# An order of 4345 steps, its first 1753 arranged anew

## The chip, the cores and the metric

The kernel runs on one core of a Trainium2 chip. The metric is the device time of one execution in microseconds: the median of three runs of the kernel before is 1051.68 us (1048.98 to 1051.96). A profiled execution gives the start and end of every instruction on the five engines: TensorE (PE, with its weight loads as PEld), VectorE (DVE), ScalarE (ACT), GpSimd (POOL) and SyncE (SP), which issues every transfer of this kernel.

## What is computed

A transformer block on x of shape (8, 512, 512): attention with 16 heads of width 32 and a causal mask, then a feed-forward layer with quantised activations and ternary weights.

```python
x = x + layernorm(attention(layernorm(x)))      # eps 1e-5
x = x + layernorm(ffn(x))

# attention: q, k, v = split(x @ w_attn + b_attn), rotary turn of q and k that depends on the head
p = softmax(where(causal, q @ k.T, -inf)) * 512**-0.5
out = (p @ v) @ w_proj + b_proj

# ffn: two "bitlinear" layers with a gelu between (512 -> 2048 -> 512)
xn = layernorm(x)                                # eps 1e-6
x_hat = clip(xn * 128 / absmax(xn), -128 + 1e-6, 128 - 1e-6) * absmax(xn) / 128
w_hat = sign(round(w / (mean(abs(w)) + 1e-6))) * mean(abs(w))
y = x_hat @ w_hat.T
```

## The kernel before

The batch has eight images of 512 rows; rows are worked in tiles of 128, so there are 32 row tiles (b, c). Products that need more than half precision are formed from a high and a low f16 part, in three passes or with both parts as operands. The work is written as Python generators, one for each piece of work, and a letter names the stream that a generator belongs to. Each `yield` ends a *step*: a few instructions, mostly of one engine.

- `n`, `N`: load a row tile (`load_x`, L491), normalise it, split it in halves and transpose it (`prepare_x`, L496). In the first image PE transposes; later a transfer does, into xT.
- `w`, `H`, `J`, `B`, `R`, `I`: load and prepare the weights of attention. `t`, `T`, `Y`: load the sixteen pieces of the two feed-forward weights (`load_piece`, L406), sum their magnitudes (`magnitude`, L426) and make them ternary (`ternarize`, L461), half of it on DVE.
- `Q`: queries and keys of four heads (`queries_keys`, L565), twelve steps for one group, six of them for each of two PSUM tiles: matmuls (L575), eviction on ACT (L587) and DVE (L589). `V`: values of half the heads for a row tile (`values`, L538), four steps: two of matmuls (L545), ACT (L558), DVE (L560).
- `S`: scores of four heads (`maxima`, L596), nine steps for one block: three matmul steps (L610), each followed by two DVE steps (L624) that add the mask, take the extremum and empty PSUM into the tile p.
- `A`: probabilities (`probabilities`, L646): exponentials on ACT (L661), a cast to f16 on ACT (L667), the difference on POOL (L669), and then a transposing transfer of ph into pT. Each block has four such transfers, two of 128x24x128 and then two of 128x16x128 elements.
- `W`: the weighted sum of values (`weighted`, L682), seven steps for a pair of heads; the third and sixth read the smaller pT (L696). `G`: gather four heads, split and transpose them into oT. `r`, `P`: load the residual rows and project (`project`, L736; eight steps for a row tile, matmuls L741).
- `F`: the first quantisation (`ff_front`, L792), whose transfer makes qT of 128x8x128. `X`: the expansion (`ff_expand`, L817): matmuls L827, gelu on ACT L836. `Z`: the second quantisation (`ff_quantise`, L845), with two transfers of 128x16x128 into qT. `C`: the contraction (`ff_contract`, L876), fourteen steps for a row tile: eight of matmuls (L883), then statistics, output row and its store.

A letter and a number mean a step of a stream, counted from 0: A331 is the 332nd step of stream A.

What sets the order is the string `ORDER` (L36), 4345 letters. The kernel goes through it and lets the named stream take its next step; `pin` (L952) then ties every instruction to the one before it on the same engine, so that each engine executes in exactly this order:

```python
for k in "".join(ORDER.split()):
    step(k)
```

So an engine that waits holds up all that stands behind it in its own queue, and nothing else. SP's queue has loads, stores and transposing transfers in one line. Buffers are few: two PSUM tiles for the products of Q, V, P and C (`mm`), three larger ones for scores and the expansion (`sc`), three score tiles p, two each of ph and pT in either size.

All transposing transfers are issued here (L521):

```python
def transpose(dst, q):
    nc.sync.dma_start_transpose(
        out=dst.rearrange("p h k q -> p (h k) q"), in_=q.rearrange("p h f -> p (h f)")
    )
```

Of the kernel before, what the change touches and what calls it, by code (L numbers as in the profile page):

```python
# [33 lines left out]


ORDER = """  # L36
nNNNwHIwHHHNwJJNJNNnNHJBBBBBBBBBNNNNRHJJwRRRNNBNBnNHHHNNHHRwJJtHJNNJHRBtnNwwJNJtRHHBBRNNHRNNTJTH
JHJJNNTNRtNtTTtTtTHNNQHQQQQHJnJNtTJHNwYHQYYHYNYQYJQQQHwBYYHQtYYHQJJQHYYQQJSSBTQYYQSQQYYQQHQSSAAQ
AAQVYAAVtVJtYAAAttSSVAQYQAQtQSAAQQQAQJSAAQAABBQQAAAVJSVVAAAQJSAVSVVVVJRVVSAVVVVSAAAVAVnrSVTSQQVA
TVQVAAWNSnQVVQAQWrWWVnWWnQAAAVVTAVQTQQNNNNAWWWWWSWANAWVNNNAAAAAASNNNNNWSSRAATAQAAAASNAWWQNASAANA  # L40
VNVVWWWASGGAAASSWWSWWWWWWAAAAVVVGVAVSVSASNAVVVVAAANAANAWQAAQQQSQSAAAnQGQQGAAWQGSSSQWWWWAAVQAAQVS
WWWWWWWAAVAAAAAQWVAAQRRRRRRQSSAQSSAtWWWQAtASQSQQQAWAQWGGWWWGAVArAWQWQWWWWWASSASAQAVQTQVAATYVQYYY
GGGSSAAAAQQYYYYQQQSQAAAQYAAAPPPPPQPYWPWSSPVPAVPWVVFWWWWPPnAVPASFSFAAAASAAASPVVVAYPYAAAFFQQQQSSQW
WWFWWQWAAAASWAQQAAFAAYQQVSVNNYPSAAANVAVFSYQXAAANNNFAFAAXXXNXNXXAFFXQrnXXGPPFSSNNPPNWGWPVWNNWWAWA
WWVWWWWSPAAAAWVVAAAAVVVASZSYANNNAASFVYVVZArPYYPVAZXWZAAAVFnXXXXXFPXZAAXPXXSSAAAZZZQPGQPQSSWPSQQF
GWZWQQWSWQWAGWAZWWZQWQAWQWCGWZACAQAAQAWSSSAAZAAAQQQQQACAGAAAGASZZCWCWCSAAAVCVVGAAZCSSVQCSCWCWFWQ
WSWQWQAWWWWAAAAACVCWVQQFAAVQSVVZQWVAAASPVVPGQWSZAQQQQFGGNPQAZSSCQAAPQAAQQWWWWNWAAZZXZZVnXWAVANVV
AAAAPSAZXVFFPFZVVPSPNAZZnXASQSWQWWVQWQWAAPWPAZQAAWAQXQQQSQNNCQNSFNXCSAXQAXNnNANAASSFFXPZAXPZZWNr
NANSNNFCWWAWWWCPnGCZGWFPWCPPFWAANWWCZAAANWNWNSPSZZAAAVCVVVCWACAAZACXSCFXVXVXVVPQFSVQSAFFFZVAAAVQ
VZNSFZZXPXAAQQQQXFXQXFAXNQSZPQWPWSPXPWXCCZQWWZZAZZAPCAXFAACQWZPAAZCAPrXCAXZSFZFFZPPCFPSPSCPCXGGC  # L50
XXGWWWWWWGAAXASZZCCACPZWVZANCCCCZrVFCZXSFZVVZWCASQCZWAQAAAAACAQGAAFGSCQQCSCQQWNQWWWZWZZGSAAQCPXA
WQWWWWWWXAPCAAAAACCVSAAQWFZXVVGQVVFSXVSSXVVCrGVZFZXPGVPXSXPFZFFAZAVVQAPQASPAPQAAAAAAAAAWWSQQQQnZ
ZFXXCQCZQAZZCQQCSSCWFWFWWWCAAWWQWWWASCZVWPAVAACWZVSFVQCQnXPZAQFSAXXAZQAAZCZCACCSPASSAPAACASACAZA
XQAAQPXZXPXXPCXPQWWZZFGCZZWQWWQWGXZAZWQXCFAZAXWCWCAWWAWWCPrFNFNXNCQPQVCANAXFZnPFFNXVXNNWSNNAXZZX
ZCCZCSCPNVNCXCPVSSrNZCPnZZZZNCXAXAPZZAZZAFXACAPVNCNNAVSAPSZCXASZCVAVAAAVCZAAZSSAAVVCVSQZPCCASAAA
AXCQCWWSQVCPQVXXWQQWXQWVFVNWQCrPAZQPZZZQPGGGXAPGFZZAQWSQXAQPSCWWAWQWWWACQASNXFACFZZFQCAAASWFCZWW
CAAZAQFQQCGGSXCFQWPWZZZXWWPSAAAAAGAQNFACXACAQAZWSFFFXCSACVWWVnWWWZAAQSQPFXXZZWVXXWAAGVVNXFXSQZAG
FXAQVVSQAGSSZQXXZQCCZVVQZAAAAZQFVQAXSQVVAWFCFFQAZCWZACQAQPCPZXSCSCWPCWPCASXWrAZWZAZZPZZXXZAAAAFA
# [986 lines left out]
```

## Time and profile before

| what | value |
|---|---|
| median of three runs | 1051.68 us (1048.98 to 1051.96) |
| the profiled execution | 1051.51 us |
| its span, first to last instruction | 1049.7 us |
| mean granted PE clock | 0.978 |
| PE busy | 977.2 us, 93% |
| ACT busy | 904.8 us, 86% |
| DVE busy | 855.8 us, 82% |
| POOL busy | 759.7 us, 72% |
| transfers from SP's queue, share of 16 DMA engines | 90.2% |
| transposing transfers | 284: 128 into pT, 96 into qT, 32 into oT, 28 into xT |

The busy time of an engine is the time in which an instruction of it runs; waiting for a semaphore or issuing a transfer is not busy. For a transfer the profile gives two times: how long SP's queue was held by its issue, and when it landed. Step 1753 of the order, the first behind the rearranged part, starts on PE at 414 us of the span.

### The profile page before, as it was taken

To read this page: it belongs to the slowest core of one execution; us is meant where nothing else is said; L and a number is where in the kernel's file an instruction comes from. 1 tells how busy PE (TensorE), PEld (TensorE's weight loads), DVE (VectorE), ACT (ScalarE), POOL (GpSimd) and SP (SyncE) were. 2 spreads that over 40 slices of the span, in tenths; PEclk is the share of its full clock that TensorE was granted. 3 is DMA by queue.
4 is the path that set the end of the run, shared out by engine and by line. 5 is a ranking of instruction groups with operands and counts; after the bars stand their busy time and mean duration, and the time that the engine had idled before them with its cause. 6 is when DMAs were issued, how large, how long until landed. Compare 5 with 4: busy or idle time off the path is not lost.

```text
span 1049.7 us, 22994 instructions
## 1 busy us (share of the span) xinstructions
PE 977.2 (93%) x8258; PEld 511.0 (49%) x8258; DVE 855.8 (82%) x2674; ACT 904.8 (86%) x1502; POOL 759.7 (72%) x608
## 2 busy tenths in 40 slices
PE   5787888899999999999999999999999999999995
PEld 4544544445555555555545455454454454544442
DVE  7898789989998888887988897888778888866752
ACT  5789998999999998999899999889999889964552
POOL 5249875888877778877888688677967678865544
PEclk9898899999999999999999999999999999999998
DMA  9369998999999988999999999989999879995553
GB/s 308 111 143 205 185 222 128 183 185 194 192 188 181 163 177 163 201 176 183 178 196 177 170 192 178 167 160 192 185 169 175 171 142 170 198 193 110 110 101 80
DMA packets 585027, 181.10 MB, mean 173 GB/s; under 512 B 564304, under 2 KB 568400, under 8 KB 584912
## 3 DMA queue, kind: packets, MB, share of 16 engines
q1 hardware_dynamic: 584912, 179.63, 90.2%
q8 instruction: 64, 1.05, 0.4%
q14 instruction: 51, 0.42, 0.1%
HBM read 29.64 MB, written 8.39 MB: 36 GB/s over the span
## 4 chain that ended last, share of the span: by engine, by line
PE 26%; ACT 25%; DVE 18%; DMA 11%; POOL 10%; issue 9%; SPq 1%; POOLq 0%; ACTq 0%; DVEq 0%
PE sc L827 7%; ACT p L661 6%; PE mm L883 6%; DVE p L624 5%; POOL ph L669 4%; DMA pT<-ph 4%; DMA qT<-q 4%; PE mm L575 4%; ACT ph L667 3%; PE mm L545 2%; PE sc L696 2%; ACT junk L865 2%; ACT h L836 2%; PE mm L741 2%; ACT L836 2%
## 5 line engine op out<-in xcount | busy, mean ns | idle before, releaser
L669 POOL TENSOR_TENSOR ph<-p,ph 128x768 f16<-128x768 f32 (+1 forms) x192 | 355.7, 1856 | 112.8 <-ACT ph L667 92.6
L624 DVE CUSTOM_DVE_ANT_0 p<-sc,mask,e_scale 128x384 f32<-128x384 f32 (+3 forms) x512 | 255.4, 546 | 25.1 <-POOL ph L669 13.2
L883 PE MATMUL mm<-wout,qT 128*128 128x512 fp8e4 x1024 | 260.1, 383 | 6.6 <-ACT row L901 5.1
L827 PE MATMUL sc<-wfc,qT 128*128 128x512 fp8e4 x1024 | 254.6, 379 | 3.9 <-DVE low L624 1.9
L661 ACT ACTIVATE p<-p,nmax 128x384 f32<-128x384 f32 (+3 forms) x512 | 253.5, 552 | 3.0 <-DVE nmax L635 2.5
L575 PE MATMUL mm<-xT,wqk 128*128 128x512 f16 x768 | 203.6, 384 | 2.2 <-DVE vt L560 1.3
L667 ACT CAST ph<-p 128x768 f16<-128x768 f32 (+1 forms) x192 | 172.4, 898 | 5.0 <-DMA pT<-ph 2.0
L827 PEld LDWEIGHTS <-qT 128*128 128x128 f16 x1024 | 96.6, 98 | 117.6 <-issue 9.7
L883 PEld LDWEIGHTS <-qT 128*128 128x128 f16 x1024 | 95.1, 98 | 115.3 <-issue 15.3
L696 PEld LDWEIGHTS <-pT 128*128 128x128 f16 x2560 | 97.1, 98 | 51.6 <-issue 11.9
L575 PEld LDWEIGHTS <-wqk 128*128 128x128 f16 x768 | 70.4, 98 | 83.2 <-issue 16.8
L545 PE MATMUL mm<-wv,xT 128*128 128x256 f16 x768 | 105.1, 278 | 5.8 <-DVE src L589 3.7
L696 PE MATMUL sc<-vt,pT 128*128 128x65 f16 (+1 forms) x2560 | 100.3, 187 | 10.9 <-DMA pT<-ph 4.5
L741 PE MATMUL mm<-wp,oT 128*128 128x512 f16 x384 | 103.2, 381 | 0.8 <-DVE src L589 0.8
L861 POOL TENSOR_SCALAR h<-h,hnm,hqs 128x1024 f32<-128x1024 f32 x64 | 80.1, 1252 | 30.4 <-DVE hnm L857 28.8
L545 PEld LDWEIGHTS <-xT 128*128 128x128 f16 x768 | 73.9, 99 | 37.0 <-issue 11.0
L610 PE MATMUL sc<-src 32*128 32x128 f16 (+3 forms) x1536 | 74.8, 298 | 16.9 <-DVE low L624 9.8
L783 POOL TENSOR_TENSOR q<-h,q 128x1024 f16<-128x1024 f32 x32 | 68.7, 2146 | 24.0 <-ACT q L778 20.1
L865 ACT ACTIVATE junk<-h 128x1024 bf16<-128x1024 f32 x64 | 67.2, 1050 | 16.5 <-DMA qT<-q 12.7
L850 DVE TENSOR_REDUCE htop<-h 128x1 f32<-128x1024 f32 x64 | 76.3, 1211 | 4.6 <-ACT h L836 4.5
L778 ACT CAST q<-h 128x1024 f16<-128x1024 f32 x64 | 66.6, 1040 | 13.2 <-POOL h L861 11.8
L836 ACT ACTIVATE h<-sc,fsc 128x1024 f32<-128x1024 f32 x64 | 71.1, 1111 | 1.9 <-PE sc L827 1.5
(161 smaller groups left out, 1380.8 us busy)
## 6 DMA issues: line engine op xcount, KB each, us to landing
row<-in_x SPq DMA_DIRECT2D x32, 256.0 KB, 3.6
x<-in_x SPq DMA_DIRECT2D x32, 256.0 KB, 3.2
out<-row SPq DMA_DIRECT2D x32, 256.0 KB, 2.7
tw<-in_w_fcT SPq DMA_DIRECT2D x8, 512.0 KB, 8.3
tw<-in_w_outT SPq DMA_DIRECT2D x8, 512.0 KB, 4.4
wraw<-in_w_attn SPq DMA_DIRECT2D x8, 256.0 KB, 4.8
pT<-ph SPq DMA_TRANSPOSE x128, 5.6
qT<-q SPq DMA_TRANSPOSE x96, 4.3
```

Source lines behind the costliest of these rows:

```text
L545: nc.tensor.matmul(ps[:, :256], xT[:, c, hx, k, :], wv[hw][:, k, half * 256 : (half + 1) * 256], start=(n == 0), stop=(n == 3 * NE - 1),)
L575: nc.tensor.matmul(ps, w[:, hw, k, :], xT[:, :, hx, k, :], start=(n == 0), stop=(n == 3 * NE - 1),)
L624: nc.vector.tensor_tensor_reduce(p[:, j, at : at + (i + 1) * P], scs[t][:, j, at : at + (i + 1) * P], mask[:, T - (i + 1) * P :], e_scale[ ...
L661: nc.scalar.activation(pj, pj, AF.Exp, bias=nm[:, i, 2 * t + j : 2 * t + j + 1], scale=-1.0)
L667: nc.scalar.copy(hi, p)
L669: nc.gpsimd.tensor_tensor(lo, p, hi, ALU.subtract)
L696: nc.tensor.matmul(oo[:, j, i, :width], probs[u, PARTS[i]][:, half, j, STARTS[i] + c, :], vt[c][:, h, :width], start=(n == 0), stop=(n == ...
L741: nc.tensor.matmul(ps, oTs[b, k][:, ho, i, :], wp[hw][:, k, :], start=(n == 0), stop=(n == 3 * NE - 1),)
L827: nc.tensor.matmul(ps[:, o1, :], xsT[0][:, n // NE, n % NE, :], wfc[:, n % NE, ts(o, 512)], start=(n == 0), stop=(n == 2 * NE - 1),)
L836: nc.scalar.activation(h[:, ts(o2, 1024)], ps.rearrange("p a f -> p (a f)"), AF.Gelu, scale=xsc, accum_out=hsum[:, o2 : o2 + 1],)
L865: nc.scalar.activation(junk, hh, AF.Square, accum_out=hsq[:, o2 : o2 + 1])
L883: nc.tensor.matmul(ps, hT[0][:, half, k, :], wout[:, o2 * NF // 2 + k, :], start=(n == 0), stop=(n == 2 * NF - 1),)
```

## The change

The first 1753 letters of `ORDER` (steps 0 to 1752) are another arrangement of the same letters; from step 1753 on the string is the same. Each stream still takes its own steps in its own order, so instructions, tiles, buffers and transfers are the same, and only the interleaving of the streams differs. The arrangement was made with a different account of how long a transfer holds its queue (a shorter time). At no place does a stream run ahead of or behind its old place by more than some steps: after 1000 letters, for instance, A has taken 213 steps instead of 214, Q 120 instead of 122, S 84 instead of 83. The lines of the string that differ, whole:

```diff
@@ ORDER @@
-nNNNwHIwHHHNwJJNJNNnNHJBBBBBBBBBNNNNRHJJwRRRNNBNBnNHHHNNHHRwJJtHJNNJHRBtnNwwJNJtRHHBBRNNHRNNTJTH
-JHJJNNTNRtNtTTtTtTHNNQHQQQQHJnJNtTJHNwYHQYYHYNYQYJQQQHwBYYHQtYYHQJJQHYYQQJSSBTQYYQSQQYYQQHQSSAAQ
-AAQVYAAVtVJtYAAAttSSVAQYQAQtQSAAQQQAQJSAAQAABBQQAAAVJSVVAAAQJSAVSVVVVJRVVSAVVVVSAAAVAVnrSVTSQQVA
-TVQVAAWNSnQVVQAQWrWWVnWWnQAAAVVTAVQTQQNNNNAWWWWWSWANAWVNNNAAAAAASNNNNNWSSRAATAQAAAASNAWWQNASAANA
-VNVVWWWASGGAAASSWWSWWWWWWAAAAVVVGVAVSVSASNAVVVVAAANAANAWQAAQQQSQSAAAnQGQQGAAWQGSSSQWWWWAAVQAAQVS
-WWWWWWWAAVAAAAAQWVAAQRRRRRRQSSAQSSAtWWWQAtASQSQQQAWAQWGGWWWGAVArAWQWQWWWWWASSASAQAVQTQVAATYVQYYY
-GGGSSAAAAQQYYYYQQQSQAAAQYAAAPPPPPQPYWPWSSPVPAVPWVVFWWWWPPnAVPASFSFAAAASAAASPVVVAYPYAAAFFQQQQSSQW
-WWFWWQWAAAASWAQQAAFAAYQQVSVNNYPSAAANVAVFSYQXAAANNNFAFAAXXXNXNXXAFFXQrnXXGPPFSSNNPPNWGWPVWNNWWAWA
-WWVWWWWSPAAAAWVVAAAAVVVASZSYANNNAASFVYVVZArPYYPVAZXWZAAAVFnXXXXXFPXZAAXPXXSSAAAZZZQPGQPQSSWPSQQF
-GWZWQQWSWQWAGWAZWWZQWQAWQWCGWZACAQAAQAWSSSAAZAAAQQQQQACAGAAAGASZZCWCWCSAAAVCVVGAAZCSSVQCSCWCWFWQ
-WSWQWQAWWWWAAAAACVCWVQQFAAVQSVVZQWVAAASPVVPGQWSZAQQQQFGGNPQAZSSCQAAPQAAQQWWWWNWAAZZXZZVnXWAVANVV
-AAAAPSAZXVFFPFZVVPSPNAZZnXASQSWQWWVQWQWAAPWPAZQAAWAQXQQQSQNNCQNSFNXCSAXQAXNnNANAASSFFXPZAXPZZWNr
-NANSNNFCWWAWWWCPnGCZGWFPWCPPFWAANWWCZAAANWNWNSPSZZAAAVCVVVCWACAAZACXSCFXVXVXVVPQFSVQSAFFFZVAAAVQ
-VZNSFZZXPXAAQQQQXFXQXFAXNQSZPQWPWSPXPWXCCZQWWZZAZZAPCAXFAACQWZPAAZCAPrXCAXZSFZFFZPPCFPSPSCPCXGGC
-XXGWWWWWWGAAXASZZCCACPZWVZANCCCCZrVFCZXSFZVVZWCASQCZWAQAAAAACAQGAAFGSCQQCSCQQWNQWWWZWZZGSAAQCPXA
-WQWWWWWWXAPCAAAAACCVSAAQWFZXVVGQVVFSXVSSXVVCrGVZFZXPGVPXSXPFZFFAZAVVQAPQASPAPQAAAAAAAAAWWSQQQQnZ
-ZFXXCQCZQAZZCQQCSSCWFWFWWWCAAWWQWWWASCZVWPAVAACWZVSFVQCQnXPZAQFSAXXAZQAAZCZCACCSPASSAPAACASACAZA
-XQAAQPXZXPXXPCXPQWWZZFGCZZWQWWQWGXZAZWQXCFAZAXWCWCAWWAWWCPrFNFNXNCQPQVCANAXFZnPFFNXVXNNWSNNAXZZX
-ZCCZCSCPNVNCXCPVSSrNZCPnZZZZNCXAXAPZZAZZAFXACAPVNCNNAVSAPSZCXASZCVAVAAAVCZAAZSSAAVVCVSQZPCCASAAA
+nNwHwHHwJNNNNJNNHHJJnnBBBBRBBBBBNNNNNJwHRRRBNHNHHtNJNNTHHJRBwJJJNtHHNtwwNBBBHNRNJnRJNJHRHTNNTHNJ
+nHRRJJJtwttIHNtNNNQNNHNTQJJQTTTNHHtTYwJJJQYYYJHHHQYYQYYBQQHHQQQYYQQHtYYQTNQSStYYSQnQQAQQANYAYBQQ
+QStHYSQAVVAJYASASQAVQVAYSAAQAABQQQAnQBQQAQAAQSJSQJSAAVAAVVVSVVAAJVVVAAVAJSVVttnVAAASntVVAAAATVSV
+SQVVTVQWSQRQQVQWVAAWVWWAAQWQVVQQTVANNSNATNWNWWNNWNWWAAAAAAWSVAANNNNANWTSASAAAAANNWSWQVVANVRWNSWA
+AAAWWSSAAQGGASWWSAWWWWAAAWAVVVVASVVSSAGVANAAAQVVQNVAQAAAAWNSSQQQQQrQQASAAnQQSQWWWWrAAWWAAQVVGSQS
+GWAAWWWWWAAVAAAAQQAASVRRRGRRQWASASARttQQQWQQQAAWVWSSWWWWSAAGGWWWWWWWWAVASQSQAQAASGSQAAVATTYVYYAY
+SGGGAAAAQYQYQQQQYYSPPAAPAAPSAPSWQYAPAPWVVVQYPPnVFAAWPWWWWFAVPFPAPVAAASAAVVSQFSFSPAYYAAQAQrQrQQQS
+SQWQWWWWWWPFQVVAANAASSAANYPYAVAASFFAGQNVAAAAANNnNNYSFAFAXAXXXANXXXXXAXFNNPNNPSSPWPPWQWWWWFFSGWWV
+WWAVWWAYAWAANAVVVVSSAAZSAAVAVPAPZYYNFNVVNAYXAAXZVPZAAAAXXXXZPXXPWXXVSPFAFAGGGSAZQWFQZSWWQPGPQQWW
+WSWAZZAAAZQQZQWAAZSSWQWWQQQWAAAAACWCZSWSZAQCGAQSrSZnnAZAASAAZACAAQCQQQAGSGAACCCCWAAWVVVSVSPFWWCP
+FCWAQSWAWQWWAAQQCWCWWAAVQVQNAWVVASSAWSAZAVAQVZVGVFQQQAQSWQWPFQPWQAGWWWSWQNAZGnZXAQXXASSAAACAAAAA
+QQPAAANVPZNZSVVWSWPWWWAVQAPWFQFVWQAFZZAZZVQPXZAVVCPQQQSQCQCAQXXNNNNSAPSCSNZCXNANSWnAAANFAnCFWQFr
+XNQPXFCPWNNAFANWAWAASXGZWGWPCPASWWNNAZZPVWSWVWXNANCWACXXFZZZZZAVVVAAAAXCVCASVPQAAWSVPQVASQXXSVPV
+VAAXQXPXSFQQPFZXQFPWWWFPCCQAFZAZAWZSFXWQFFPCXQCAZZAZZAWCAXCrAAAQXCFPZZXNNFFASFQZPPPAZCFFSSZCPCXA
+CAPGXXPGAZZCCCCSPrGWWWWWWZVWZWZCCFZXAAAGVWCXVASWVQCQZAAACAAQCQFACQGZZSSSZQCQSCXQWWXQWWGFGAAXAAAA
+CZSZNWCCWWQWWWWAAAAAPZCVXQWVXCVFGSFQVVZrZAXPVPZXVVPVXVASSGGAFZZXVVPSQPAAQPQFSWPAAAAAAAZCSQQCQWCQ
+CQZZCWWWQWXNFCSAACQZAZCWWSAZWWAWFWnZZAAQAAAAAWQVCPSVSVWZVXAQAAAPSGAXAZZACQXCQSCSCAQSQQXQPAWWCQPQ
+AXPQPXFrSWXAACWPWWGXPWCWWZFFCXCZAWAAAAQFQNAZFNFnZCWVZZNAAXXANWCNZFXCZWZNXNZPCWZFnZFPXFCNCNNnPCCX
+XVVXSVXCPNXNZZZCPCCPSZSrSZZZNCXAXAPZZAZZAFXACAPVNCNNAVSAPSZCXASZCVAVAAAVCZAAZSSAAVVCVSQZPCCASAAA
```

## The prediction

> **What bounds the kernel now.** First the page's span and busy times, then its 40 slices:
>
> ```profile
> span 1049.7 us, 22994 instructions
> PE 977.2 (93%) x8258; PEld 511.0 (49%) x8258; DVE 855.8 (82%) x2674; ACT 904.8 (86%) x1502; POOL 759.7 (72%) x608
> ...
> PE   5787888899999999999999999999999999999995
> ...
> PEclk9898899999999999999999999999999999999998
> ```
>
> PE is full from about the ninth slice on and only there: what is lost lies in the first 210 us and the last 80. To size it I read the busy times of four stretches; 414 us is where PE comes to step 1753, the first that both orders share again.
>
> ```profile
> 50.00:250.00 200.00, 169.99 (x1786) 96.33 (x1786) 178.41 (x599) 181.14 (x322) 151.73 (x107) 0.94 0.98 182
> 250.00:414.00 164.00, 162.05 (x1418) 83.81 (x1416) 140.57 (x439) 153.42 (x252) 129.21 (x104) 1.00 0.97 178
> 414.00:900.00 486.00, 479.14 (x4111) 245.30 (x4110) 408.82 (x1273) 456.11 (x739) 376.61 (x291) 1.00 0.97 178
> ```
>
> The columns are length, then busy time of PE, PEld, DVE, ACT, POOL, then granted clock, DMA share, GB/s. Up to 250 us nobody is alone the bound: PE is idle for 30.0 us of 200, DVE for 21.6, ACT for 18.9. From 250 us PE is idle for 2.0 us of 164, and after 414 us for 6.9 of 486. So a microsecond won or lost before step 1753 is passed on to the end nearly whole, and in 250 to 414 us hardly anything is left to win.
>
> Third, the waits of the first 230 us, then DVE's from 50 to 250:
>
> ```profile
> PE sc L610 <- DVE low L624: 9.8, 9, 2.1
> PE mm L545 <- DVE src L589: 3.7, 3, 2.5
> ...
> DVE p L624 <- POOL ph L669: 5.6, 5, 1.8
> ```
>
> PE waits for PSUM that DVE has to empty, not for transfers. Fourth, how long a transposing transfer keeps SP's queue (ns, min/median/max) and its way to landing:
>
> ```profile
> L523 SPq DMA_TRANSPOSE pT<-ph x128: 1602/3564/5278, 69.4 to 928.7; - x128
> L523 SPq DMA_TRANSPOSE xT<-hT x28: 1231/1269/2542, 93.5 to 755.9; - x28
> ...
> pT<-ph SPq DMA_TRANSPOSE x128, 5.6
> qT<-q SPq DMA_TRANSPOSE x96, 4.3
> ```
>
> **The change, part by part.** *Added or removed:* nothing. The letters up to step 1752 are the same multiset, and there are 72 table loads on ACT in both, so no engine's total changes; the cost is only in who arrives late. I summed, from the rows of the trace, the work each engine has ahead of a given step in either order, and read the clock off the trace: when had this engine done so much? That tells which moved pair no longer fits; it gives no total by itself.
>
> *Setup and first stretch (steps 0 to 975).* Three of eight loads of the second weight, not six, precede the first score transfers. Cost on SP: they are moved past four pT transfers, but queue and DMA were idle about then (61 to 69 us), so nothing, unless a reader comes early: the first magnitude step that reads a moved load is step 320, 52 steps behind the load. DVE sets this stretch: at the fourth S block (step 420, now 416) it has 99.0 us of work ahead in both orders, ACT 88.1 and now 87.9, PE 65.4 in both. In between, S blocks come with up to 4.7 us less ACT work ahead and pT transfers with up to 6.5 us less DVE work, while the last pT of a group often comes with 2 to 4 us more PE work ahead. Bounds: DVE's idle time in 100 to 150 us is 10.5 us, against 3.4 in the stretches on either side, so a gain of at most 7.1 there; a loss of the same size as the longest present waits, three of 2.1 us, 6. These have no lean that I can see: 0.
>
> *Around 260 us.* C14, the first contraction matmuls of a tile, now stands right behind V95, the DVE step that frees its PSUM buffer. PE reaches C14 after 189.3 us of work, which it had done at 265.5 us; DVE starts V95 after 235.3 us, which it had done at 267.4, and takes 0.41. C14 is wanted 2.4 us before it may start. Before, V95 ended at 264.5 and C14 began at 268.8:
>
> ```profile
> 264.06 0.41 DVE L560 SCALAR_TENSOR_TENSOR vt<-mm,vt 128x256 f16<-128x256 f32 x1
> ...
> 268.77 1.03 PE L883 MATMUL mm<-wout,qT 128*128 128x512 fp8e4 x4
> ```
>
> Behind it in PE's queue stand P38 and Q136 to Q138; Q138 has the same fault (2.3 us), but is moved on with C14 and costs nothing more. PE is the bound here: **2.4 us**. Below, 0, if the first stretch leaves DVE that much ahead; above, 4.4, with the 2.0 us by which Q132 misses V91 just earlier, if DVE does not catch up.
>
> *Around 390 us.* W184 reads the pT that step A331 transposes. PE comes to W184 after 309.2 us of work instead of 312.2, at 390.2 us by the trace's clock. Its transfer stood thus (start, time in the queue):
>
> ```profile
> 388.38 2.70 SPq L523 DMA_TRANSPOSE pT<-ph  x1
> 391.13 0.58 SPq L905 DMA_DIRECT2D out<-row  x1
> 391.79 2.35 SPq L523 DMA_TRANSPOSE pT<-ph  x1
> ```
>
> and landed at 392.7. If it lands then, W184 lacks 2.5 us. But the transfers before it (A323, A327) come with less work ahead: A323 at 379.4, two large holds of 3.8 us (as at 260.06 us in the timeline), A331 at 387.0, 4.3 us to landing: 391.3, short by 1.1. I take **1.1**, since the row order puts the queue there, and add it, because scores, exponentials and subtraction behind this transfer start from PE and will be late with it. Low end 0 (PE is late already), high end 2.5.
>
> *Other shortened leads.* From the subtraction that fills a transposed tile to the matmul that reads it there were, in PE work, 15.5 us for W191 (now 5.9), 14.0 for C74 (2.9), 10.9 for X40 (2.7), 5.2 for P65 (0.9). Read on the clock, their transfers still land within 0.3 us of the need or before it; PE is behind its place in the order there. 0 each. POOL's A334 is due 3.2 us before ACT ends the cast A333; POOL is idle 21% of 250 to 414 us, so I price it at 0, with 3.2 as its upper end.
>
> *After step 1752:* the same order on every engine; 0.
>
> Sum: 0 + 2.4 + 1.1 = 3.5. The profiled execution took 1051.51 us (span 1049.7 and 1.8 around it), 0.17 below the median of 1051.68; 1051.5 + 3.5 = **1055.0 us**.
>
> **Two rules against the rows.** The first row: the queue holds above, 3.6 us median for pT, where a large one moves 128 x 24 x 128 x 2 bytes, 786 KB. The Trainium skill, Advanced Engine Details and Errata, X-Bar Transpose (TRN2), says that transposing transfers are as fast as plain ones, 350 to 400 GB/s; an estimate from that page is 2.2 us for the large one. By it A331 would be issued some 3 us earlier, the shortage at 390 us would not exist, and the sum would be 2.4, so 1053.9 us. The rows contradict that rate for this shape, so the sum keeps them. The second row:
>
> ```profile
> 100.00:110.00 10.00, 5.44 (x68) 3.60 (x67) 8.36 (x25) 9.15 (x18) 9.08 (x9) 0.67 1.27 182
> ```
>
> Here several waits of at most 2.5 us sufficed for a granted clock of 0.67, 3.3 us lost of ten. The Trainium skill, TensorE: Matmul & The Clock Gate, What's actually happening, throttles PE only after an idle window of about 3.4 us, which a lone 2.4 us wait would not fill. The row says that gathered short waits do it too; at 266 us PE is otherwise full, so I add nothing.
>
> **The rivals.**
>
> *Faster.* One mechanism: in 100 to 150 us DVE no longer waits for POOL's score halves, because S and A come with less ACT and POOL work ahead, and its idle time falls to its neighbours' 3.4 us: minus 7.1, so 1044.4 us with no later stall, 1047.9 with both. For it: the up to 4.7 us on ACT at the sixth S block. Against: at the seventh the two orders are within 0.7 us again on all engines. It decides once more than 6.7 us are gained there, or over 3.2 if DVE's lead covers C14.
>
> *No change.* The shortages are covered by shifts ahead of them: 1051.5 us, 1048.4 to 1054.8 counting as no change (about 0.3%, what a measurement of this kernel can tell). For it: differences of a few steps only, equal totals. Against: PE has 2.0 us of slack in 250 to 414.
>
> *Slower by more.* The shortages do not cover one another: 2.4 at C14, 2.0 at Q132, 3.2 at A334 and 2.5 at W184 make 10.1: 1061.6 us; with a disturbed first stretch somewhat above. For it: the in-order queues, where a late subtraction on POOL holds SP's next transfers. Against: POOL's idle share.
>
> **How the numbers follow.** Slower by over 0.3%: the forecast 0.29 and the larger loss 0.18, together 0.47. No change 0.26. Faster 0.27. The point is the forecast's, 1055.0. The range 1045 to 1063 reaches from the faster rival to past the larger loss and leaves a tenth out on each side; the forecast's own range is 1052 to 1058 (0 to 6.9 us, its terms' ends).
>
> **What would show it.** In the profile after: PE waiting 2 to 3 us at the first L883 matmul of a group near 266 us for DVE's L560; a wait of about 1 us of L696 for a pT transfer near 390; PE idle for some 5 us instead of 2.0 between 250 us and step 1753; that step 3 to 4 us later than 414; the rest as long as before. It is wrong if step 1753 comes earlier (then look at DVE's idle time in 100 to 150 us), or if the stretch after it changes its length.

## The result and the profile after

The changed kernel takes 1063.69 us (median of six runs, 1060.06 to 1066.29) against 1050.53 us (six runs, 1048.98 to 1052.73): a ratio of 1.0126, 95% interval 1.0108 to 1.0144. It is slower by 13.2 us; the forecast was 3.3 us over the median it started from, and the range ended at 1063. The profiled execution of after took 1066.29 us, at a mean granted clock of 0.971; it is the slowest of the six and has the lowest clock of them, so what its trace shows as lost is somewhat more than the 13.2 us of the medians.

The page after, span, busy times and slices, and then the same stretches that were read before (length, busy time of PE, PEld, DVE, ACT, POOL, granted clock, DMA share, GB/s):

```profile
span 1064.5 us, 22983 instructions
PE 981.0 (92%) x8258; PEld 511.0 (48%) x8258; DVE 857.7 (81%) x2674; ACT 905.0 (85%) x1502; POOL 757.0 (71%) x608
...
PE   5887968898989999999999999999999999999995
...
PEclk9888979999999999999999999999999999999997
```

```profile
50.00:250.00 200.00, 166.03 (x1745) 94.39 (x1744) 174.30 (x581) 176.90 (x312) 148.93 (x105) 0.91 0.93 174
250.00:414.00 164.00, 153.77 (x1358) 79.69 (x1357) 136.62 (x411) 147.09 (x241) 121.39 (x98) 0.99 0.97 172
414.00:900.00 486.00, 477.24 (x4053) 243.93 (x4052) 405.02 (x1264) 449.08 (x730) 371.69 (x290) 1.00 0.95 175
```

No engine got more to do. Of the span's 14.8 us, 11.0 are PE idle (83.5 instead of 72.5 us) and 3.8 are the same matmuls at a lower clock. In 250 to 414 us PE is idle for 10.2 us instead of 2.0. After 414 us hardly anything is added: the sixteenth score block, just behind step 1753, starts on PE at 436.0 instead of 422.9 us (13.1 late), and the end is 14.8 late.

Where in the first 430 us? Multiplying PE's busy time by the granted clock gives the work done in a stretch. First before, then after, over the same four stretches:

```profile
140.00:160.00 20.00, 15.87 (x185) 8.89 (x183) 17.77 (x56) 17.20 (x28) 12.45 (x8) 0.99 1.14 210
...
180.00:245.00 65.00, 59.57 (x618) 32.68 (x617) 58.92 (x186) 60.70 (x104) 54.45 (x41) 1.00 1.08 184
245.00:300.00 55.00, 54.70 (x496) 29.23 (x495) 51.37 (x176) 52.40 (x89) 48.51 (x40) 1.00 1.06 192
300.00:375.00 75.00, 73.35 (x659) 38.24 (x658) 62.16 (x188) 70.74 (x116) 53.48 (x43) 1.00 0.97 178
```

```profile
140.00:160.00 20.00, 14.38 (x120) 6.67 (x120) 14.67 (x40) 13.20 (x21) 10.26 (x7) 0.79 0.90 198
...
180.00:245.00 65.00, 57.42 (x581) 30.66 (x580) 60.12 (x196) 60.79 (x106) 53.16 (x40) 1.00 1.02 187
245.00:300.00 55.00, 50.63 (x488) 27.25 (x490) 48.67 (x151) 48.30 (x82) 44.90 (x39) 1.00 1.04 182
300.00:375.00 75.00, 70.73 (x593) 36.12 (x593) 60.01 (x185) 66.24 (x108) 54.33 (x42) 0.98 0.98 169
```

From 140 to 160 us, 14.4 x 0.79 instead of 15.9 x 0.99: 4.3 us less work. From 180 to 245, 2.2 less. From 245 to 375, 8.1 less. Up to 127 us, by contrast, the new order is *ahead*: the fifth score block starts 5.0 us earlier than before, the seventh (174 us) 2.8 us later, the tenth (245 us) 1.9 later, the fourteenth (369 us) 14.2 later, the fifteenth 10.1. A block's own place in the order moves too, by up to 17 steps (the fifth stands 8 steps earlier, the fourteenth 11 later), so these are marks good to a few us. A gain of up to 5 us is given back within 50 us, and most of the loss falls between 245 and 370 us.

What PE waited for there, in 120 to 180 us and then in 245 to 375 us of after (us in total, times, longest):

```profile
PE sc L696 <- DMA pT<-ph: 6.0, 2, 3.7
PE sc L696 <- DVE low L624: 2.6, 3, 2.0
PE mm L741 <- DVE src L589: 2.3, 1, 2.3
```

```profile
PE sc L696 <- DMA pT<-ph: 2.1, 1, 2.1
PE sc L827 <- ACT h L836: 2.0, 1, 2.0
PE sc L827 <- DVE low L624: 1.4, 1, 1.4
PE mm L545 <- DVE vt L560: 1.3, 1, 1.3
PE mm L741 <- DMA oT<-hT: 0.9, 1, 0.9
```

Before, there is no wait for pT in either stretch. In the first, though, PE waited for other things, most of all for this:

```profile
PE sc L610 <- DVE low L624: 6.4, 5, 2.1
```

All waits of the first stretch come to 11.6 us before and 13.8 after, so late pT transfers mostly took the place of waits for DVE there. All waits of the second come to 1.7 us before and 8.6 after, in many small pieces. Over the whole program, first the line of before that the prediction did not show, then after:

```profile
PE sc L696 <- DMA pT<-ph: 4.5, 6, 1.9
```

```profile
PE sc L696 <- DMA pT<-ph: 18.1, 12, 3.7
...
PE sc L610 <- DVE low L624: 4.9, 6, 1.1
...
DVE p L624 <- POOL ph L669: 3.5, 8, 0.9
```

PE's waits for DVE's score steps have halved (9.8 before), and the weighted sum's wait for pT has grown from 4.5 to 18.1 us. That this growth is nearly the loss is partly chance: 3.9 us of it (4.9 against 1.0) lie before 120 us, where the new order gains. The transfers themselves are as they were, in the queue (ns, min/median/max) and to landing (us):

```profile
L523 SPq DMA_TRANSPOSE pT<-ph x128: 1327/3547/4690, 66.5 to 944.4; - x128
...
pT<-ph SPq DMA_TRANSPOSE x128, 5.7
qT<-q SPq DMA_TRANSPOSE x96, 4.3
```

The largest single wait, on SP's queue and on PE (start, duration):

```profile
128.79 5.80 SPq L523 DMA_TRANSPOSE pT<-ph  x2
134.64 1.72 SPq L523 DMA_TRANSPOSE oT<-hT  x1
136.47 2.02 SPq L523 DMA_TRANSPOSE pT<-ph  x1
138.59 1.74 SPq L421 DMA_DIRECT2D tw<-in_w_outT  x2
```

```profile
142.59 1.36 PE L696 MATMUL sc<-vt,pT 128*128 128x65 f16 x28 [3.75 <-DMA pT<-ph]
```

POOL had finished the source of the transfer at 136.47 by 132.1, 2.2 us earlier than before. SP, with two larger ones and an oT transfer ahead in its line, issued it only 0.6 us earlier (before: 137.1), and it landed at the old time, 142.5 against 142.6. PE had come early and stood for 3.75 us. The granted clock was 0.50 there, but this wait did not start that: it was 0.50 from 134.8 us on, 4 us before the wait began, and until 148.5. Taking all 56 pT transfers of the rearranged part, for ten instead of four the reader starts within 0.4 us of the landing; eight of the ten are the smaller ones, the last two of a block's four in SP's line.

### The profile page after: what moved, and what is told of

Its sections match the earlier page's. It is cut to its first block, busy times and chain, and to the rows that moved or that the text cites. A ratio compares the mean times of both kernels' runs of the same rounds, so it can differ in the third digit from the quotient of the medians.

```text
span 1064.5 us, 22983 instructions
## 1 busy us (share of the span) xinstructions
PE 981.0 (92%) x8258; PEld 511.0 (48%) x8258; DVE 857.7 (81%) x2674; ACT 905.0 (85%) x1502; POOL 757.0 (71%) x608
## 4 chain that ended last, share of the span: by engine, by line
PE 30%; ACT 25%; DVE 14%; DMA 11%; POOL 10%; issue 8%; SPq 1%; POOLq 0%; ACTq 0%; DVEq 0%
PE sc L827 9%; ACT p L661 7%; PE mm L883 7%; POOL ph L669 4%; PE mm L575 4%; ACT ph L667 4%; DMA pT<-ph 4%; DMA qT<-q 4%; DVE p L624 3%; PE mm L545 3%; PE sc L696 3%; PE mm L741 2%; ACT junk L865 2%; ACT h L836 2%; ACT q L778 2%
## 5 line engine op out<-in xcount | busy, mean ns | idle before, releaser
L827 PE MATMUL sc<-wfc,qT 128*128 128x512 fp8e4 x1024 | 257.5, 382 | 6.5 <-DVE low L624 2.4
L883 PEld LDWEIGHTS <-qT 128*128 128x128 f16 x1024 | 95.2, 98 | 120.1 <-issue 14.8
L696 PEld LDWEIGHTS <-pT 128*128 128x128 f16 x2560 | 98.6, 98 | 66.1 <-DMA pT<-ph 23.5
L696 PE MATMUL sc<-vt,pT 128*128 128x65 f16 (+1 forms) x2560 | 102.4, 188 | 23.5 <-DMA pT<-ph 18.1
L545 PE MATMUL mm<-wv,xT 128*128 128x256 f16 x768 | 106.2, 280 | 4.8 <-DVE vt L560 2.8
L778 ACT CAST q<-h 128x1024 f16<-128x1024 f32 x64 | 66.6, 1040 | 16.5 <-POOL h L861 15.4
```

What stands on the lines that cost most here:

```text
L545: nc.tensor.matmul(ps[:, :256], xT[:, c, hx, k, :], wv[hw][:, k, half * 256 : (half + 1) * 256], start=(n == 0), stop=(n == 3 * NE - 1),)
L696: nc.tensor.matmul(oo[:, j, i, :width], probs[u, PARTS[i]][:, half, j, STARTS[i] + c, :], vt[c][:, h, :width], start=(n == 0), stop=(n == ...
L827: nc.tensor.matmul(ps[:, o1, :], xsT[0][:, n // NE, n % NE, :], wfc[:, n % NE, ts(o, 512)], start=(n == 0), stop=(n == 2 * NE - 1),)
L883: nc.tensor.matmul(ps, hT[0][:, half, k, :], wout[:, o2 * NF // 2 + k, :], start=(n == 0), stop=(n == 2 * NF - 1),)
```

## The experiments

All kernels keep the steps of the two orders (those with halved transfers change what a step moves); at each joint of two orders a few letters are chosen so that every stream goes on where it stood. "Before" in brackets is the kernel before on the same chip.

**The new order for 512 steps, the old one behind.** The joint, against after:

```diff
 SQVVTVQWSQRQQVQWVAAWVWWAAQWQVVQQTVANNSNATNWNWWNNWNWWAAAAAAWSVAANNNNANWTSASAAAAANNWSWQVVANVRWNSWA
 AAAWWSSAAQGGASWWSAWWWWAAAWAVVVVASVVSSAGVANAAAQVVQNVAQAAAAWNSSQQQQQrQQASAAnQQSQWWWWrAAWWAAQVVGSQS
-GWAAWWWWWAAVAAAAQQAASVRRRGRRQWASASARttQQQWQQQAAWVWSSWWWWSAAGGWWWWWWWWAVASQSQAQAASGSQAAVATTYVYYAY
+GWAAWWWWWAAVAAAAQQAASVRRRGRRQWASRASSAtWWWAtASSQQQAWAQWGGWWWGAVArAWQWQWWWWWASSASAQAVQTQVAATYVQYYY
...
```

> The new order for its first 512 steps, the old one behind. Theory (pT transfers land after PE has come to the weighted sum that reads them, and these waits sit behind step 512): the changed kernel's PE was 3 to 5 us earlier at the fifth score block, so 1046 to 1049 us. Rival (the first stretch leaves the engines skewed against each other, and the loss is the later price of that early gain): 1053 to 1060 us, with the lost time between steps 512 and 1000.

Measured: 1047.86 us (1051.28), 0.9976, interval 0.9952 to 1.0001: within the theory's range, the gain itself not yet clear of noise.

**The new order for steps 512 to 1123 only**, the old one ahead and behind (joint ahead: `RRQSSAQSSAtWWWQ` becomes `RRQSSAQQQSAttQQ`).

> The old order up to step 512, the new one from there to about step 1124, the old one behind. Theory (too short leads of pT): this part lost 5.66 + 5.05 = 10.7 us in the changed kernel (score block at 127 us to the one at 268 us), so 1056 to 1062 us, and the waits of L696 for pT grow by 6 us or more. Rival (skew inherited from the first 512 steps): 1050 to 1053 us, with no more waiting for pT than before.

Measured: 1059.18 us (1051.28), 1.0068, interval 1.0046 to 1.0089. The time is the theory's, but PE's wait for pT grew by 3.6 us over before, not by 6 or more:

```profile
PE sc L696 <- DMA pT<-ph: 8.1, 9, 2.3
```

**The new order from step 1124 on only** (joint: `NSFNXCSAXQAXNn` becomes `NSFNXCCAPSCSNZ`).

> The old order up to step 1124, the new one from there to step 1752. Theory: this part lost about 8 us in the changed kernel (5.7 us behind at the score block of 268 us, 13.8 at step 1753), so 1056 to 1060 us. Rival (skew inherited from before): 1050 to 1053 us.

Measured: 1058.54 us (1051.28), 1.0076, interval 1.0051 to 1.0101, the theory's time again, with hardly more direct waiting for pT than before:

```profile
PE sc L696 <- DMA pT<-ph: 6.3, 9, 2.3
```

So most of what either part loses is not PE standing at a pT reader. The three parts give -3.4, +7.9 and +7.3, in all +11.7 against 13.2 for the whole: they nearly add, the loss lies behind step 512, in about equal halves, and the start of the new order is no loss.

**Every pT transfer at once.** If SP's transfers only came too late in the order, putting each of the 56 right behind the subtraction that fills its source should repair it. One line of the string, against after:

```diff
-WSWAZZAAAZQQZQWAAZSSWQWWQQQWAAAAACWCZSWSZAQCGAQSrSZnnAZAASAAZACAAQCQQQAGSGAACCCCWAAWVVVSVSPFWWCP
+WSWAZZAAAZQQZQWAAAZSSWQWWQQQWAAAACWCZSWSZAQCGAQSrSZnnAZAASAAZACAAQCQQQAGSGAACCCCWAAAWVVVSVSPFWWC
```

> The changed kernel, but each of the 56 pT transfers up to step 1752 stands on SP's queue right behind the subtraction that fills its source; nothing else moves on any engine. If the pT transfers come late because the new order puts them behind other transfers (issue 2 to 6 us after the subtraction in the trace): 1054 to 1060 us. If the queue is simply full, so that another transfer is late instead: 1062 to 1066 us. If the loss has nothing to do with transfers: 1063 to 1065 us.

Measured: 1102.69 us (1051.28), 1.0492, interval 1.0463 to 1.0522. All expectations fail, by far. In 180 to 430 us PE no longer waits for pT at all, but for the other transfers and what hangs on them:

```profile
PE sc L827 <- DMA qT<-q: 8.2, 3, 4.8
PE mm L883 <- DMA qT<-q: 6.2, 2, 5.8
PE mm L575 <- ACT row L901: 5.7, 1, 5.7
PE mm L545 <- DVE vt L560: 5.1, 1, 5.1
PE mm L545 <- DMA xT<-hT: 3.5, 1, 3.5
PE mm L575 <- DMA xT<-hT: 3.2, 1, 3.2
```

SP's line can be counted like an engine: the time its issues hold it, and the time its head stands waiting for a source while others behind it may be ready. Worked out from the start and hold of each issue and the end of what fills its source:

| us, held + head waiting | steps 512 to 1123 | steps 1124 to 1752 |
|---|---|---|
| before | 111.2 + 20.2 | 105.6 + 29.1 |
| after | 111.3 + 25.2 | 107.5 + 34.8 |
| every pT at once | 109.4 + 43.7 | 103.3 + 56.5 |
| readers moved back (below) | 112.9 + 19.1 | 106.1 + 46.0 |
| pT halved, old order (below) | 71.7 + 60.5 | 74.7 + 62.9 |
| pT halved, new order (below) | 69.1 + 63.6 | 74.6 + 63.0 |

A transfer that stands first in line with an unfinished source, or with both pT buffers still being read, blocks all others. With every pT at once the head waits for PE's L696 for 14.5 us of the 43.7 (after: 0) and for POOL's subtraction for 37.5 of the 56.5 (after: 3.6). The two terms together fill nearly the whole stretch in every row, in the halved kernels too, since a line with little to issue also stands with an unfinished head; so their sum tells nothing, and the held part does: 217 of some 277 us before, 146 with pT halved. In after the line holds as before and waits 5.0 and 5.7 us more, but the stretches themselves last longer by 5.1 and 7.6 us, so this does not tell cause from effect.

**The pT transfers halved, in both orders.** The low half of the probabilities is not transposed, and the weighted sum reads the high half in its place, so the matmuls keep number and shape:

```diff
-                        probs[2 * u + t, part].rearrange("p h j k q -> p h (j k) q"),
-                        q.rearrange("p h j f -> p h (j f)"),
+                        probs[2 * u + t, part][:, 0:1].rearrange("p h j k q -> p h (j k) q"),
+                        q[:, 0:1].rearrange("p h j f -> p h (j f)"),
...
-                        probs[u, PARTS[i]][:, half, j, STARTS[i] + c, :],
+                        probs[u, PARTS[i]][:, 0, j, STARTS[i] + c, :],
```

> The old order, with every pT transfer halved: only the high half of the probabilities is transposed (128x12x128 and 128x8x128), and the weighted sum reads it twice in place of high and low half; all compute instructions stay. Serves as the base of the next run. PE is full from 250 us on, so 1040 to 1050 us.

> The new order with the same halved pT transfers. Theory (the loss is waiting for pT, whose transfers take longer than the order allows): the distance between the two orders falls from 13 us to at most 4 us, or the new one wins by the 3 us of its first 512 steps. Rival (the interleaving of the compute steps itself is worse): the distance stays at 10 us or more.

Measured: 1037.14 us in the old order (0.9882, interval 0.9862 to 0.9901), below the 1040 expected, and 1035.13 in the new (0.9863, interval 0.9835 to 0.9891; before 1049.6). So the old order gains 12.5 us as well, though PE waited for pT for only 4.5 us in it. The distance of 13.2 us is gone; -2.0 is left, with overlapping intervals. How long a pT transfer holds the queue in the new order (ns, min/median/max), and the waits of PE in 245 to 375 us:

```profile
L523 SPq DMA_TRANSPOSE pT<-ph x128: 1231/1477/2351, 65.2 to 912.6; - x128
```

```profile
PE sc L827 <- ACT h L836: 1.6, 1, 1.6
PE sc L827 <- DVE low L624: 1.4, 1, 1.4
PE mm L741 <- DMA oT<-hT: 0.5, 1, 0.5
```

8.6 us of waits there have become 3.5, and PE no longer waits for pT anywhere in the program. So the new order loses against the old one only with pT transfers of full size; with halved ones the interleaving of the compute steps costs nothing that shows. The halved transfers also lower the DMA share in 300 to 375 us from 0.98 to 0.64, so this pair does not separate the queue's hold, the way to landing and the DMA engines' load.

**All late readers later.** In the new order, W steps moved back by up to 60 places; one hunk:

```diff
-FCWAQSWAWQWWAAQQCWCWWAAVQVQNAWVVASSAWSAZAVAQVZVGVFQQQAQSWQWPFQPWQAGWWWSWQNAZGnZXAQXXASSAAACAAAAA
+FCWAQSWAWQWWAAQQCWCWWAAVQVQNAWVVASSAWSAZAVAQVZVGVFQQQAQSWQWPFQPQAGSQNAZGnZXWWWWWAQXXASSAAACAAAAA
```

> The new order, but between steps 512 and 1752 the weighted sum's steps (and what hangs on them) stand so much later that PE has at least as much work between a pT transfer and its reader as in the old order (at most 9 us of it): 43 W steps move back by 4 to 60 places, SP's queue is untouched. If the order puts the readers too close behind the transfers: 1052 to 1058 us. If instead the transfers are issued too late on SP, whatever the distance in the order: 1060 to 1065 us.

Measured: 1074.22 us (1049.6), 1.0235, interval 1.0205 to 1.0265: worse, against both expectations. Block by block it is not one effect: the tenth score block starts 2.1 us ahead of before (after: 1.9 behind), the fifteenth 14.5 behind, the sixteenth 23.4.

**Only the moves before step 1124**, by up to 22 places (the hunk above is one of them).

> The new order with the readers of pT moved back as in the run before that, but only between steps 512 and 1124 (18 W steps, by 4 to 22 places). That run's score blocks were 3 to 4.4 us ahead of the changed kernel's from 150 to 250 us, and fell behind only after 350 us. If the distance in the order is what counts and the late loss came from the last moves: 1058 to 1061 us. If moving readers back always holds up what follows: 1064 us or more.

Measured: 1058.77 us (1050.53), 1.0093, interval 1.0066 to 1.0119: 4.9 us better than the new order (the intervals overlap a little), and PE's wait for pT falls from 18.1 to 9.3 us. So a few places between a transfer and its reader seem to matter, where the move is short; the last moves of the other kernel cost some 15 us. Why is open: pT's two buffers stay occupied longer when their readers come later (in that kernel 5.0 us of SP's head waits behind step 1124 are for PE's L696, in after 0), which would hold up the transfers behind, but no run isolates it.

**Which of the two sizes.** Only the larger pT halved, in both orders; then only the smaller, in the new order:

```diff
+                    hs = 2 if part else 1
...
-                        probs[2 * u + t, part].rearrange("p h j k q -> p h (j k) q"),
-                        q.rearrange("p h j f -> p h (j f)"),
+                        probs[2 * u + t, part][:, 0:hs].rearrange("p h j k q -> p h (j k) q"),
+                        q[:, 0:hs].rearrange("p h j f -> p h (j f)"),
...
-                        probs[u, PARTS[i]][:, half, j, STARTS[i] + c, :],
+                        probs[u, PARTS[i]][:, half * PARTS[i], j, STARTS[i] + c, :],
```

For the smaller the first line is `hs = 1 if part else 2` and the factor in the last `(1 - PARTS[i])`. As above, the low half of that size is left out and its high half read twice.

> The old order with only the larger pT transfers halved (128x12x128 in place of 128x24x128; the weighted sum reads their high half twice), the smaller ones whole. Base of the next run: 1040 to 1046 us.

> The new order with only the larger pT transfers halved. In the trace PE waits almost only at readers of the smaller ones, which stand last in each group of four. If that is because two larger ones stand ahead of them in SP's line: the distance to the old order falls to 4 us or less. If it is the smaller ones' own way from issue to landing (4.3 us): the distance stays at 8 us or more.

> The new order with only the smaller pT transfers halved (128x8x128 in place of 128x16x128). With the larger ones halved it came to 1043.3 us. If the larger ones ahead in the line were what PE waited for, halving the smaller ones gives back less: 1052 to 1060 us. If both sizes only count by the time that they take from the line (the larger ones some 1.9 us each, these 1.2), 1048 to 1053 us. At 1043 or less the smaller ones' own way counts most.

Measured: larger halved, old order 1041.62 us (0.9919, interval 0.99 to 0.9938), new order 1043.33 (0.9927, interval 0.9902 to 0.9952; before 1050.53): 1.7 us apart. Smaller halved, new order 1040.7 (0.9898, interval 0.987 to 0.9927; before 1051.02). The pT holds in the new order, larger halved and then smaller halved:

```profile
L523 SPq DMA_TRANSPOSE pT<-ph x128: 1273/1785/3598, 63.8 to 923.8; - x128
```

```profile
L523 SPq DMA_TRANSPOSE pT<-ph x128: 1231/2777/5497, 67.5 to 920.6; - x128
```

I had thought that the smaller transfers are late *because* two large ones stand ahead of them. Halving the large ones does remove the loss, but halving the small ones brings the new order as far down, 1040.7, so the "because" does not stand: either relief seems to be enough. For the smaller ones the old order was not run; if halving them alone does no more for it than halving both (1037.14 us), the new order is at most 3.6 us behind.

**The first 512 steps again**, since that kernel might beat both: the same file, more rounds.

> The new order for its first 512 steps and the old one behind, again, with more rounds: the only version that may beat both. If its gain is real: 0.2 to 0.4% below the kernel before, with the interval below 1; if not, 0.998 to 1.002.

Measured: 1047.21 us (twelve runs, 1044.04 to 1049.86; before 1050.53), 0.9972, interval 0.9959 to 0.9986. It is the fastest kernel here that computes the whole: 3.3 us under before and some 16 under after. It also warns against adding up one wait: in the profiled execution of the first of the two, PE waits 12.7 us for pT, 8.2 more than before, 7.1 of the 12.7 before 120 us, and this order is still no slower.

## Why the prediction was wrong

- **What bounds the kernel.** Half right. PE is full from 250 us on and a delay up to step 1753 does reach the end (13.1 us late there, 14.8 at the end). What I did not do is count SP as an engine. SP shows no busy time, but in steps 512 to 1752 its issues hold its line for 217 us (the table's first row) of the 277 between PE's steps 517 (137 us) and 1753 (414), and the DMA share of about 1 stood in the lines I showed. "PE waits for PSUM that DVE has to empty, not for transfers" was true of before and was exactly what the new order changed.
- **Setup and first stretch, "no lean that I can see: 0".** The net was small (+1.9 us by the tenth score block) and within the bounds of -7.1 and +6, but as two large terms: -5.0 up to 127 us and +6.9 behind. The first 512 steps alone gain 3.3 us, about half of what the rival that ended faster had, but not by its mechanism: in 100 to 140 us of that kernel's first profile DVE is idle for 10.6 us, before for 8.6.
- **C14 behind V95, 2.4 us.** Did not occur. V95 ends 5.4 us ahead of C14:

```profile
265.75 0.42 DVE L560 SCALAR_TENSOR_TENSOR vt<-mm,vt 128x256 f16<-128x256 f32 x1
...
271.56 1.03 PE L883 MATMUL mm<-wout,qT 128*128 128x512 fp8e4 x4
```

- **W184 behind A331's transfer, 1.1 us.** The place was right, the size was 0.4 us: PE was itself late by then.

```profile
401.47 0.39 PE L696 MATMUL sc<-vt,pT 128*128 128x65 f16 x8 [0.37 <-DMA pT<-ph]
```

- **"Other shortened leads ... 0 each".** This is the step that failed. From the tenth to the sixteenth score block 11.2 us are lost, where I had 3.5 from two other places. I read the leads on the old trace's clock, "their transfers still land within 0.3 us of the need or before it": a margin of nothing, for transfers whose time of issue depends on everything ahead of them in SP's line. Of the four pairs that I priced at 0, two did wait: P65 0.9 us for its oT at 369 us, C74 1.2 us for its qT at 413; W191 and X40 did not. The largest wait for pT between 245 us and step 1753, W114 with 2.1 us at 255, was at a pair that I had not looked at, and the rest is a string of waits for DVE and ACT. That the zero fails through the size of the pT transfers is what the halved pair shows (13.2 us apart with full transfers, -2.0 with halved ones); by which chain is not shown. Errors of this kind are probably one-sided: where PE is full, a transfer that comes early has little to win, and one that comes late costs.
- **The larger loss, 1061.6 us.** Near in size, but its places (C14, Q132, A334, W184) were not the ones, so it was not right either.
- **After step 1752: 0.** Right to 1.7 us: one new wait of 2.2 us for pT at 593 us, and small changes both ways.
- **The two rules.** An estimate by the rate in the Trainium skill, Advanced Engine Details and Errata, X-Bar Transpose (TRN2), made the sum 1053.9 us, further off than the rows' 1055.0; the rows' 3.8 us for 786 KB are some 207 GB/s. With the larger transfers at half their size the new order is 1.7 us behind the old, not 13.2. For the clock, the row that I read as 3.3 us lost holds half clock from 99.4 to 106.2 us, with PE busy for 3.8 of them: 1.9 us. After, the clock was at half for 17.1 us of 120 to 180, before for 10.2; but PE stood idle for much of it, and half of its busy time in these stretches is 5.4 against 5.0 us, so the clock explains little of the loss there. The Trainium skill, TensorE: Matmul & The Clock Gate, What's actually happening, puts its idle window at about 3.4 us; these traces agree with the length but not with "idle" (the last section has the numbers).

What stays open is which property of a pT transfer does it (hold, way to landing, or load on the DMA engines), and which single chain makes the 8.6 us of waits in 245 to 375 us.

## What to carry to other kernels

An in-order queue that issues the transfers is an engine: add up what its issues hold, and if that is most of a stretch (here 217 us of 277), a new order has to be judged by that line too, though the profile calls it never busy. An order made with too short a hold looks tight and loses on the chip; with shorter transfers it was as good as the old one. And late transfers were not repaired by issuing all of them earlier (39 us worse) or reading all of them later (10.5 us worse); a few short moves gave 4.9 us back. Try the order in pieces, as the first 512 steps were worth keeping.

## What was not expected of the hardware

- Putting the issues of 56 transfers right behind the work that fills their sources, and nothing else, cost some 39 us (1102.69 against 1063.69).
- Halving the larger transfers alone, 64 of the 128, took away 11.5 us of a 13.2 us difference between two orders. Halving the smaller ones alone brought the new order to 1040.7 us; the old one was not run so.
- The granted clock of before and after is only ever 1.00 or 0.50, and the stretches at 0.50 last 3.4 us or a multiple of it. PE was never idle for the whole of the 3.4 us ahead of a fall: in the 21 falls of the two traces it was busy for 0.5 to 1.8 us of them, and no such stretch that kept the full clock had less than 1.6 (worked out from the times at which the clock changes and PE's busy time).
